# Layer 2: expert rows and router logits made group by group inside softmax attention, and row factors in place of two norms

## The chip, the cores and the metric

The kernel runs on one core of a Trainium2 chip. A core has a matrix engine (PE), a vector engine (DVE), an activation engine (ACT), a general engine (POOL) and a queueing engine (SP)[...]. They meet in on-chip memory (SBUF) and in the accumulator banks (PSUM) that PE writes. The metric is the device time of one execution in microseconds (us); the time before is the median of three runs.

## The reference, cut to what matters

The model has four layers over `x` of 2 sequences of 1024 rows with 128 features. Each layer computes `x = x + s * silu(f)` from the same `xn = layernorm(x)`, where `s` comes from a mixing branch and `f` from an expert branch. Layer 2, the only one that the change touches, is:

```python
# mixing branch: linear attention, 16 heads of 8
x_norm = (xn - mu) / sqrt(var + 1e-05) * ln_g + ln_b
q, k, v = split(x_norm @ w_qkv + b_qkv)
gate_sig = sigmoid(xn @ w_gate + b_gate)
gate_norm = gate_sig / (mean(gate_sig) + 1e-05)
q, k = elu(q * gate_norm) + 1, elu(k * gate_norm) + 1
out = (q . cumsum(k v)) / (q . cumsum(k) + 1e-05)
s = out @ w_proj + b_proj
# expert branch: softmax attention, then 2 of 8 experts
h = xn + attention(rms_norm(xn, norm1_w))      # rope, 16 query heads in 4 groups
logits = rms_norm(h, norm2_w) @ router_w + router_b
f = h + sum over the 2 chosen experts of weight * expert(rms_norm(h, norm2_w))
```

`rms_norm(x, w)` is `x / sqrt(mean(x * x) + 1e-06) * w`. The rope turns even features `xe` and odd features `xo`: `[xe*cos - xo*sin, xe*sin + xo*cos]`.

## The kernel before, in words

The 2048 rows lie as 16 tiles of 128 rows, `[128, 16, 128]` in SBUF; four tiles are a group (`G = 4`, groups 0 to 3), eight are a sequence. `layer2` works in three stages.

*Preparation.* `K.normalise` (L320) takes mean and variance of each group's rows on DVE (`moments`: L310, L311, then `rsqrt` L299 to L301, whose square root is on ACT), makes `xn`, and transposes it into `xT` on PE (L293). Then `Attention.prepare` runs for each sequence: the sum of squares of `xn` by ACT (`sumsq`, L333), its reciprocal root, `xw = xn * factor * norm1_w` on DVE (L1352), the rope as six POOL products and sums of 128x256 per group (L1360 to L1365), transposes of the turned rows `xr`, and the query, key and value products. PE starts on attention when the first sequence's two groups are there.

*Softmax attention* (`softmax_attention`). PE's order is written out by hand (`manual_schedule`): 72 steps, one for each block of 128 rows against 128 rows, 36 for each sequence. In a step PE makes score maxima's inputs in `pm` banks (pool `sm2`, three banks, all under the tag "pm"), DVE reduces each to `mx` (L1424), PE makes the scores `psc` (two buffers), ACT takes the exponential `pr` (L1468), and PE multiplies it by the values into `pat`. When a tile of rows is complete, `close` normalises it, projects it (`pho`) and adds it to `xn`: that is `h` (L1505), one tile after another; the last is tile 15. Parts that fall due in a later step are kept in the dictionary `later`. The other engines' orders come from a scheduler.

*Experts, with linear attention beside them.* After the last `h`, for each group: sum of squares of `h` on ACT (L333), its reciprocal root `rs`, `hn = h * rs * norm2_w` on DVE (L1031), a DMA of the four tiles of `hn` by SP into a table of rows in HBM (`keep_rows`, L1219), four transposes and a copy into `hnT` (L282 or L284, ACT and DVE in turn). The router's `logits` are 16 matmuls of 128x8 (`plg`) and one add into `lg` (L393). `top2` (its first maximum is `rm`, L364) and `Dispatch` make from them the places of each row (`dto`) and the rows of each place (`dfrom`, L1176). `d.n` = 23 blocks of experts follow (L1048 to L1078): two gathers of rows by POOL with `dfrom` (`xb`, L1188), their transpose, first products `p`, gate `sg` on ACT (L1069) and product `hh` on DVE (L1070), second product `po`, `yb` (L1076), and a scatter (L1198). `linear_attention` is a generator that the block loop advances at blocks 0, 0, 11 and 22. For each group it takes the second layer norm of `xn` again (`moments` with tag "la": L310, L311, `lars`; `xl`, L1242), transposes it (`pxl`, `xlT`), and makes `pqg` in two matmuls, 384 columns from `xlT` and 128 from `xT`; then `qg = pqg + bq` (L1255), the sigmoid `sig` with its sum (L1256), `qk` (L1263), the exponential (L1265), the products `kv` (L1280), their running sums `pcum` by matmul, `prod` (L1286) and the quotient.

Of the kernel before, what the change touches and what calls it, by code (L numbers as in the profile page):

```python
# [19 lines left out]
P = 128  # L20
# [252 lines left out]
class Kern:  # L273
# [46 lines left out]
    def normalise(self, pool, ps, x, xn, xT, xs=None):  # L320
        for g in range(NG):
            mv, rs = self.moments(pool, lambda j: x[:, g * G + j, :], G, 1e-5, "ln")
            for j in range(G):
                i = g * G + j
                self.nc.vector.tensor_scalar(xn[:, i, :], x[:, i, :], mv[:, j, 0:1], rs[:, j : j + 1], ALU.subtract, ALU.mult)  # L325
# [50 lines left out]
    def pair_softmax(self, pool, m1, m2):  # L376
# [9 lines left out]
        return w, d  # L386

# [606 lines left out]
def layer2(K, x, xn, xT, w, inp):  # L994
# [3 lines left out]
    with ExitStack() as es:  # L998
        keep = es.enter_context(tc.tile_pool(name="k2", bufs=1))
        s = keep.tile([P, NT, P], F32, name="s")  # L1000
        h = keep.tile([P, NT, P], F32, name="h")
        with ExitStack() as e1:
            pf = e1.enter_context(tc.tile_pool(name="f2", bufs=1))
            seqs = [Attention(K, pf, xn, w, h, b) for b in range(NB)]
            with tc.tile_pool(name="sn2", bufs=8, space=PSUM) as sn, tc.tile_pool(name="p2", bufs=1) as pp:
                K.normalise(pp, sn, x, xn, xT)
                for a in seqs:
                    a.prepare(pp, sn)
# [3 lines left out]
            with tc.manual_schedule(engines={mybir.EngineType.PE}):  # L1012
                with ExitStack() as e3:
# [3 lines left out]
                    softmax_attention(K, pf, sm, sc, so, seqs)  # L1017
        with ExitStack() as e2:
# [4 lines left out]
            hT = pf.tile([P, T], F32, name="hnT")  # L1023
            rs = pf.tile([P, NT], F32, name="rs")
            hn = pf.tile([P, NT, P], F32, name="hn")
            for g in range(NG):
                for i in range(g * G, g * G + G):
                    K.sumsq(pf, rs[:, i : i + 1], h[:, i, :])
                K.rsqrt(rs[:, g * G : (g + 1) * G], rs[:, g * G : (g + 1) * G], 1.0 / P, 1e-6)
                for i in range(g * G, g * G + G):  # L1030
                    nc.vector.scalar_tensor_tensor(hn[:, i, :], h[:, i, :], rs[:, i : i + 1], w["n2"], ALU.mult, ALU.mult)  # L1031
                keep_rows(K, inp["lists"][0], hn, g)
                K.to_feature_major(sf, lambda i: hn[:, i, :], hT, g)
            with tc.tile_pool(name="r2", bufs=1) as pr:
                (m1, h1), (m2, h2) = K.top2(pr, K.logits(pr, sf, hT, w["wr"], w["br"], 8), 8)
# [3 lines left out]
            linear = linear_attention(K, pa, sa, xn, xT, w, s)  # L1039
# [182 lines left out]
def linear_attention(K, pa, sa, xn, xT, w, s):  # L1222
# [7 lines left out]
    wq, bq = two("wq", [P, 384]), two("bq", [P, 512])  # L1230
# [4 lines left out]
    nc.vector.tensor_scalar_mul(wq, w["wqkv"], w["g"])  # L1235
# [595 lines left out]
```

## Time and profile before

| what | value |
|---|---|
| median of the runs | 1370.8 us (1363.27, 1370.8, 1372.84) |
| profiled execution: its own time, and its span | 1371.2 us, 1369.3 us |
| mean granted PE clock | 0.887 |
| busy share of the span: PE, DVE, ACT, POOL | 83%, 65%, 46%, 31% |
| layer 2: first rotation on POOL, first mask of attention, last `h` written | 490.99, 530.4, 843.84 us |
| layer 2: `lg` added, `dfrom` ready, first expert product `p` | 863.19, 911.34, 919.65 us |

All durations come from the profiled execution, whose span starts at 0; its own time is 1.9 us longer than its span. A line of the profile names the source line, the engine, the operation, then output and inputs by their names in the program with the shapes; "idle before" is how long the engine stood still in front of an instruction, and the arrow names what ended that. In a line in order of time the first number is the start, the second the duration; several instructions of one kind in a row are put together, with their count after "x". [...]

### The profile page before, as it was taken

How to read it: one execution, taken by the hardware profiler on the slowest of the kernel's cores; microseconds unless marked ns; L12 is line 12 of the kernel's file. 1: busy time of each engine (PE TensorE's matmuls, PEld its weight loads, DVE VectorE, ACT ScalarE, POOL GpSimd, SP SyncE). 2: the span in 40 equal slices, each digit the busy share in tenths (PEclk: the TensorE clock that was granted, in tenths of full speed). 3: DMA queues.
4: the chain of work that ended last, by engine and by line, in shares of the span. 5: the costliest groups of instructions: out<-in, count | busy, mean ns of one | idle time of the engine just before them, and what ended most of it. 6: DMA issues, size and time to landing. Idle time of an engine off the chain costs nothing. (4 is left out here: it accounts for less than half of the span.)

```text
span 1369.3 us, 19321 instructions
## 1 busy us (share of the span) xinstructions
PE 1134.2 (83%) x6861; PEld 793.5 (58%) x6861; DVE 885.1 (65%) x2216; ACT 634.7 (46%) x1072; POOL 425.2 (31%) x420
## 2 busy tenths in 40 slices
PE   5599866888898748999999998679989918799985
PEld 2277455787798425544444433458778815577664
DVE  6536445875665686577787753988657469566456
ACT  7665926215413232344455576233452316355761
POOL 0352160027455150000000000034766521467743
PEclk9899885899999757699999998769999967799997
DMA  2000003014344200000000000024344530233411
GB/s 89 0 1 1 0 15 122 1 59 157 105 136 134 62 0 1 1 1 1 1 1 1 1 1 24 8 89 117 111 131 126 155 104 24 70 85 96 78 54 47
DMA packets 49040, 75.72 MB, mean 55 GB/s; under 512 B 7335, under 2 KB 36402, under 8 KB 48688
## 3 DMA queue, kind: packets, MB, share of 16 engines
q1 hardware_dynamic: 39632, 54.30, 12.7%
q0 software_dynamic: 8448, 14.98, 5.0%
q10 hardware_dynamic: 864, 5.21, 1.1%
q8 instruction: 54, 0.88, 0.3%
q14 instruction: 42, 0.34, 0.1%
HBM read 63.95 MB, written 12.85 MB: 56 GB/s over the span
## 5 line engine op out<-in xcount | busy, mean ns | idle before, releaser
L1424 DVE TENSOR_REDUCE mx<-pm 128x1 f32<-128x512 f32 (+3 forms) x304 | 182.1, 656 | 65.6 <-PE pm L287 62.6
L1468 ACT ACTIVATE pr<-psc 128x1024 f32<-128x1024 f32 x144 | 139.6, 1021 | 103.9 <-PE psc L287 68.2
L1188 POOL DMA_INDIRECT xb<-xs,dfrom x132 | 131.7, 998 | 123.2 <-PE pxb L797 31.5
L1198 POOL DMA_INDIRECT ys<-yb,dto x132 | 137.0, 1038 | 95.3 <-DVE yb L1076 44.4
L1163 POOL TENSOR_TENSOR dhh<-dhh,w_c 128x1280 fp32r<-128x1280 f32 (+2 forms) x3 | 8.8, 2927 | 480.3 <-issue 385.6
L287 PE MATMUL pm<-kT,qT 32*128 32x128 f32 (+3 forms) x576 | 119.3, 364 | 15.5 <-DVE mx L1424 11.4
L287 PEld LDWEIGHTS pm<-kT,qT 32*128 32x128 f32 x576 | 68.8, 203 | 68.3 <-DVE mx L1424 48.2
L287 PE MATMUL p<-xbT,tw 128*128 128x256 f32 x368 | 100.6, 391 | 1.7 <-ACT sg L1069 1.4
L1069 ACT ACTIVATE sg<-p,tw 128x256 f32<-128x256 f32 x92 | 40.8, 472 | 94.9 <-PE p L287 87.2
L287 PE MATMUL pat<-pr,va 128*32 128x512 f32 x576 | 81.0, 630 | 0.2 <-ACT pr L1468 0.2
L293 PE MATMUL tp<-w_c,xn 128*128 128x128 f32 x64 | 19.5, 412 | 67.7 <-DVE xn L325 40.3
L287 PEld LDWEIGHTS p<-xbT,tw 128*128 128x128 f32 x368 | 63.4, 194 | 12.3 <-ACT sg L1069 3.5
L287 PE MATMUL psc<-qT,kT 32*128 32x512 f32 x288 | 64.8, 487 | 3.0 <-ACT pr L1468 3.0
L1070 DVE SCALAR_TENSOR_TENSOR hh<-p,tw,sg 128x256 f32<-128x256 f32 x92 | 42.6, 479 | 35.6 <-ACT sg L1069 24.0
L287 PEld LDWEIGHTS po<-tw,hh 128*128 128x128 f32 x368 | 54.6, 193 | 5.8 <-DVE hh L1070 1.1
L287 PE MATMUL po<-tw,hh 128*128 128x128 f32 x368 | 56.7, 277 | 0.4 <-DVE hh L1070 0.4
L293 PEld LDWEIGHTS tp<-w_c,xn 128*128 128x128 f32 x64 | 11.5, 187 | 75.8 <-issue 38.7
L287 PE MATMUL psc<-mT,onesR 32*128 32x512 f32 x288 | 54.5, 410 | 0.0
L282 ACT COPY xbT<-pxb 128x256 f32<-128x256 f32 (+3 forms) x38 | 15.2, 401 | 61.0 <-PE pxb L797 44.9
L287 PEld LDWEIGHTS psc<-qT,kT 32*128 32x128 f32 x288 | 31.4, 188 | 15.9 <-ACT pr L1468 13.6
L287 PE MATMUL pcum<-kv,w_c 128*128 128x512 f32 x64 | 35.3, 652 | 2.1 <-DVE prod L1286 1.6
L287 PE MATMUL pd<-uda,w_c 128*128 128x512 f32 x64 | 34.9, 647 | 0.9 <-ACT usz L517 0.9
(531 smaller groups left out, 2840.6 us busy)
## 6 DMA issues: line engine op xcount, KB each, us to landing
tw<-in_rows SPq DMA_DIRECT2D x23, 836.0 KB, 4.8
tw<-in_rows SPq DMA_DIRECT2D x39, 384.0 KB, 3.2
yt<-ys SPq DMA_DIRECT2D x24, 256.0 KB, 3.0
tw<-in_rows SPq DMA_DIRECT2D x47, 128.0 KB, 2.2
xb<-xs,dfrom POOLq DMA_INDIRECT x132, 3.3
ys<-yb,dto POOLq DMA_INDIRECT x132, 2.3
xs<-xn SPq DMA_DIRECT2D x8, 256.0 KB, 2.3
w_l<-in_l ACTq DMA_DIRECT2D x1, 1890.0 KB, 11.1
```

Of the source, the lines that this page charges most:

```text
L282: self.nc.scalar.copy(out, in_)
L287: self.nc.tensor.matmul(out, lhsT=lhsT, rhs=rhs, start=start, stop=stop)
L293: self.nc.tensor.transpose(pt[:, j, :], src(g * G + j), self.c["ident"])
L1069: nc.scalar.activation(sg, p1[:, k - k0, :], AF.Silu, bias=t[:, 1536 + k : 1537 + k])
L1070: nc.vector.scalar_tensor_tensor(hh[:, k, :], p2[:, k - k0, :], t[:, 1540 + k : 1541 + k], sg, ALU.add, ALU.mult)
L1163: nc.gpsimd.tensor_mul(h, h.bitcast(F32), c["slot"][:, at].unsqueeze(2).to_broadcast(shape))
L1188: self.K.nc.gpsimd.indirect_dma_start(dst, None, self.xs, bass.IndirectOffsetOnAxis(self.of_token[:, n : n + 1], 0))
L1198: d = self.K.nc.gpsimd.indirect_dma_start(self.ys, bass.IndirectOffsetOnAxis(self.to[:, n : n + 1], 0), src, None, bounds_check=2 * T - 1, ...
L1424: nc.vector.tensor_reduce(mx[:, starts.index(a), g, j : j + k], tile[0][:, : k * m].rearrange("p (j m) -> p j m", m=m), AX.X, ALU.max)
L1468: K.nc.scalar.activation(pr, ps, AF.Exp, scale=scale)
```

## The change

In preparation, `normalise` also keeps the mean square of each normalised row, `ms = variance * rs * rs`. `prepare` takes the root of that in place of the sums of squares; `norm1_w` is multiplied into four rope tables (cos and sin, for even and odd features) once on POOL, and `xw` becomes a scaled copy on ACT. The linear attention's own layer norm is left out: since `xn` has zero mean, its factor is `r2 = 1 / sqrt(ms + 1e-5)`, a number per row, applied after the product. So `pqg` is one matmul of 512 columns from `xT`, and `qg` is an add of 128 columns and a multiply-add of 384.

After attention's `h`, the rows `hn`, their DMA, their transposes and the router's logits are made group by group: groups 0 and 1 get their factors and rows at step 42, group 2 at step 52 (`norm`); transposes come at steps 45, 47 and 55 and logits at 48, 50 and 58, in `pm` banks, put into `later` through the new argument `fill`. Group 3 follows attention as before. The tiles `hT`, `rs`, `lg` and `hn` move to a pool that is open during attention, `hn` with two buffers of a group each.

```diff
@@ -317,9 +317,12 @@
         self.nc.vector.tensor_mul(out, mv[:, :, 1], rs)
         self.nc.vector.tensor_mul(out, out, rs)
 
-    def normalise(self, pool, ps, x, xn, xT, xs=None):
+    def normalise(self, pool, ps, x, xn, xT, xs=None, ms=None):
         for g in range(NG):
             mv, rs = self.moments(pool, lambda j: x[:, g * G + j, :], G, 1e-5, "ln")
+            if ms is not None:
+                self.mean_squares(ms[:, g * G : (g + 1) * G], mv, rs)
             for j in range(G):
                 i = g * G + j
                 self.nc.vector.tensor_scalar(xn[:, i, :], x[:, i, :], mv[:, j, 0:1], rs[:, j : j + 1], ALU.subtract, ALU.mult)
@@ -384,6 +387,14 @@
         nc.vector.reciprocal(w, w)
         nc.vector.tensor_mul(d, d, w)
         return w, d
+    def group_logits(self, ps, tag, lg, xT, g, w, bias, E):
+        pl = ps.tile([P, G, E], F32, name="plg", tag=tag)
+        for j in range(G):
+            i = g * G + j
+            self.mm(pl[:, j, :], xT[:, i * P : (i + 1) * P], w)
+        self.nc.vector.tensor_add(grp(lg, g), pl, bias.unsqueeze(1).to_broadcast([P, G, E]))
 
     def logits(self, pool, ps, xT, w, bias, E):
         pl = ps.tile([P, NT, E], F32, name="plg", tag="ps")
@@ -999,13 +1010,46 @@
         keep = es.enter_context(tc.tile_pool(name="k2", bufs=1))
         s = keep.tile([P, NT, P], F32, name="s")
         h = keep.tile([P, NT, P], F32, name="h")
+        hT = keep.tile([P, T], F32, name="hnT")
+        rs = keep.tile([P, NT], F32, name="rs")
+        lg = keep.tile([P, NT, 8], F32, name="lg")
+        r2 = keep.tile([P, NT], F32, name="r2")
+        normed = {}
+        def norm(gs):
+            for i in range(gs[0] * G, gs[-1] * G + G):
+                K.sumsq(keep, rs[:, i : i + 1], h[:, i, :])
+            at = slice(gs[0] * G, gs[-1] * G + G)
+            K.rsqrt(rs[:, at], rs[:, at], 1.0 / P, 1e-6)
+            for g in gs:
+                normed[g] = keep.tile(four, F32, name="hn", bufs=2)
+                for j in range(G):
+                    i = g * G + j
+                    nc.vector.scalar_tensor_tensor(normed[g][:, j, :], h[:, i, :], rs[:, i : i + 1], w["n2"], ALU.mult, ALU.mult)
+                nc.sync.dma_start(inp["lists"][0].rearrange("(i p) d -> p i d", p=P)[:, g * G : (g + 1) * G, :], normed[g])
+        def hidden_columns(g, ps, tag):
+            pt = ps.tile(four, F32, name="tp", tag=tag)
+            for j in range(G):
+                nc.tensor.transpose(pt[:, j, :], normed[g][:, j, :], c["ident"])
+            K.copy(hT[:, g * G * P : (g + 1) * G * P], flat(pt))
         with ExitStack() as e1:
             pf = e1.enter_context(tc.tile_pool(name="f2", bufs=1))
             seqs = [Attention(K, pf, xn, w, h, b) for b in range(NB)]
+            ms = keep.tile([P, NT], F32, name="ms")
             with tc.tile_pool(name="sn2", bufs=8, space=PSUM) as sn, tc.tile_pool(name="p2", bufs=1) as pp:
-                K.normalise(pp, sn, x, xn, xT)
+                n1 = w["n1"].rearrange("p (f two) -> p f two", two=2)
+                turn = {}
+                for n, a in (("cos", 0), ("sin", 0), ("cos", 1), ("sin", 1)):
+                    turn[n, a] = pp.tile([P, TPB, 64], F32, name=f"{n}{a}")
+                    nc.gpsimd.tensor_mul(turn[n, a], w[n], n1[:, :, a].unsqueeze(1).to_broadcast([P, TPB, 64]))
+                K.normalise(pp, sn, x, xn, xT, None, ms)
+                K.rsqrt(r2, ms, 1.0, 1e-5)
                 for a in seqs:
-                    a.prepare(pp, sn)
+                    a.prepare(pp, sn, ms, turn)
             pl = e1.enter_context(tc.tile_pool(name="l2", bufs=1))
             for a in seqs:
                 a.loop = pl
@@ -1014,29 +1058,28 @@
                     sm = e3.enter_context(tc.tile_pool(name="sm2", bufs=3, space=PSUM))
                     sc = e3.enter_context(tc.tile_pool(name="sc2", bufs=2, space=PSUM))
                     so = e3.enter_context(tc.tile_pool(name="so2", bufs=1, space=PSUM))
-                    softmax_attention(K, pf, sm, sc, so, seqs)
+                    half = TPB * (TPB + 1) // 2
+                    mid = half + G * (G + 1) // 2
+                    routed = [(half + 6, lambda: norm([0, 1])), (mid + 6, lambda: norm([2]))]
+                    for g, s0 in ((0, half + 9), (1, half + 11), (2, mid + 9)):
+                        routed.append((s0, lambda g=g: hidden_columns(g, sm, "pm")))
+                        routed.append((s0 + 3, lambda g=g: K.group_logits(sm, "pm", lg, hT, g, w["wr"], w["br"], 8)))
+                    softmax_attention(K, pf, sm, sc, so, seqs, routed)
         with ExitStack() as e2:
             pa = e2.enter_context(tc.tile_pool(name="a2", bufs=1))
             pf = e2.enter_context(tc.tile_pool(name="m2", bufs=1))
             sa = e2.enter_context(tc.tile_pool(name="sa2", bufs=3, space=PSUM))
             sf = e2.enter_context(tc.tile_pool(name="sf2", bufs=5, space=PSUM))
-            hT = pf.tile([P, T], F32, name="hnT")
-            rs = pf.tile([P, NT], F32, name="rs")
-            hn = pf.tile([P, NT, P], F32, name="hn")
-            for g in range(NG):
-                for i in range(g * G, g * G + G):
-                    K.sumsq(pf, rs[:, i : i + 1], h[:, i, :])
-                K.rsqrt(rs[:, g * G : (g + 1) * G], rs[:, g * G : (g + 1) * G], 1.0 / P, 1e-6)
-                for i in range(g * G, g * G + G):
-                    nc.vector.scalar_tensor_tensor(hn[:, i, :], h[:, i, :], rs[:, i : i + 1], w["n2"], ALU.mult, ALU.mult)
-                keep_rows(K, inp["lists"][0], hn, g)
-                K.to_feature_major(sf, lambda i: hn[:, i, :], hT, g)
+            norm([NG - 1])
+            hidden_columns(NG - 1, sf, "ps")
+            K.group_logits(sf, "ps", lg, hT, NG - 1, w["wr"], w["br"], 8)
             with tc.tile_pool(name="r2", bufs=1) as pr:
-                (m1, h1), (m2, h2) = K.top2(pr, K.logits(pr, sf, hT, w["wr"], w["br"], 8), 8)
+                (m1, h1), (m2, h2) = K.top2(pr, lg, 8)
                 d = Dispatch(K, pf, pr, sf, h1, h2, 8, 2 * P, inp["lists"])
                 w12 = K.pair_softmax(pf, m1, m2)
             pe = e2.enter_context(tc.tile_pool(name="e2", bufs=1))
-            linear = linear_attention(K, pa, sa, xn, xT, w, s)
+            linear = linear_attention(K, pa, sa, xT, r2, w, s)
             turns = [0, 0, d.n // 2, d.n - 1]
             loaded = {}
 
@@ -1219,7 +1262,7 @@
     K.nc.sync.dma_start(xs.rearrange("(i p) d -> p i d", p=P)[:, g * G : (g + 1) * G, :], grp(src, g))
 
 
-def linear_attention(K, pa, sa, xn, xT, w, s):
+def linear_attention(K, pa, sa, xT, r2, w, s):
 
 
 
@@ -1227,32 +1270,25 @@
     four = [P, G, P]
     two = lambda n, shape, bufs=1: pa.tile(shape, F32, name=n, tag=n, bufs=bufs)
 
-    wq, bq = two("wq", [P, 384]), two("bq", [P, 512])
+    wq, bq = two("wq", [P, 512]), two("bq", [P, 512])
     pb = sa.tile([P, 384], F32, name="pb", tag="ps")
     K.mm(pb, w["b"].to_broadcast([P, P]), w["wqkv"])
     nc.vector.tensor_add(bq[:, :384], pb, w["bqg"][:, :384])
     nc.scalar.copy(bq[:, 384:], w["bqg"][:, 384:])
-    nc.vector.tensor_scalar_mul(wq, w["wqkv"], w["g"])
+    nc.vector.tensor_scalar_mul(wq[:, :384], w["wqkv"], w["g"])
+    nc.scalar.copy(wq[:, 384:], w["wg"])
     for g in range(NG):
         first = g % (NG // NB) == 0
         kvs = nc.vector if g < NG // NB else nc.gpsimd
-        xl = two("xl", four)
-        mv, rs = K.moments(pa, lambda j: xn[:, g * G + j, :], G, 1e-5, "la")
-        for j in range(G):
-            nc.vector.tensor_scalar(xl[:, j, :], xn[:, g * G + j, :], mv[:, j, 0:1], rs[:, j : j + 1], ALU.subtract, ALU.mult)
-        pt = sa.tile(four, F32, name="pxl", tag="ps")
-        for j in range(G):
-            nc.tensor.transpose(pt[:, j, :], xl[:, j, :], c["ident"])
-        xlT = two("xlT", four)
-        K.copy(xlT, pt)
         qg = two("qg", [P, G, 512], 2)
         sig, gsum = two("sig", four), two("gsum", [P, G])
         for j in range(G):
             i = g * G + j
             pq = sa.tile([P, 512], F32, name="pqg", tag="ps")
-            K.mm(pq[:, :384], xlT[:, j, :], wq)
-            K.mm(pq[:, 384:], xT[:, i * P : (i + 1) * P], w["wg"])
-            nc.vector.tensor_add(qg[:, j, :], pq, bq)
+            K.mm(pq, xT[:, i * P : (i + 1) * P], wq)
+            nc.vector.tensor_add(qg[:, j, 384:], pq[:, 384:], bq[:, 384:])
+            nc.vector.scalar_tensor_tensor(qg[:, j, :384], pq[:, :384], r2[:, i : i + 1], bq[:, :384], ALU.mult, ALU.add)
             nc.scalar.activation(sig[:, j, :], qg[:, j, 384:], AF.Sigmoid, accum_out=gsum[:, j : j + 1])
 
         kvs.memset(qg[:, :, 384:400], 1.0)
@@ -1335,7 +1371,7 @@
         self.K.nc.scalar.copy(high, src)
         self.K.nc.vector.scalar_tensor_tensor(dst, high.bitcast(F32), low, src, ALU.mult, ALU.add)
 
-    def prepare(self, pp, sc):
+    def prepare(self, pp, sc, ms, turn):
         K, pf, xn, w, b = self.K, self.pf, self.xn, self.w, self.b
         nc, c = K.nc, K.c
         four = [P, G, P]
@@ -1344,24 +1380,22 @@
         for g in range(TPB // G):
             tiles = range(b * TPB + g * G, b * TPB + g * G + G)
             gr = rs[:, g * G : (g + 1) * G]
-            for j, i in enumerate(tiles):
-                K.sumsq(pp, gr[:, j : j + 1], xn[:, i, :])
-            K.rsqrt(gr, gr, 1.0 / P, 1e-6)
+            K.rsqrt(gr, ms[:, tiles.start : tiles.stop], 1.0, 1e-6)
             xw = pp.tile(four, F32, name="xw", bufs=2)
             for j, i in enumerate(tiles):
-                nc.vector.scalar_tensor_tensor(xw[:, j, :], xn[:, i, :], gr[:, j : j + 1], w["n1"], ALU.mult, ALU.mult)
+                nc.scalar.activation(xw[:, j, :], xn[:, i, :], AF.Copy, scale=gr[:, j : j + 1])
             pair = xw.rearrange("p t (f two) -> p t f two", two=2)
             xe, xo = pair[:, :, :, 0], pair[:, :, :, 1]
             at = slice(g * G, g * G + G)
-            cos, sin = w["cos"][:, at, :], w["sin"][:, at, :]
+            cose, sine, coso, sino = (turn[n, a][:, at, :] for a in range(2) for n in ("cos", "sin"))
             xr = pp.tile(four, F32, name="xr", bufs=2)
             t2 = pp.tile([P, G, 64], F32, name="t2", bufs=2)
             t3 = pp.tile([P, G, 64], F32, name="t3", bufs=2)
-            nc.gpsimd.tensor_mul(xr[:, :, :64], xe, cos)
-            nc.gpsimd.tensor_mul(t2, xo, sin)
+            nc.gpsimd.tensor_mul(xr[:, :, :64], xe, cose)
+            nc.gpsimd.tensor_mul(t2, xo, sino)
             nc.gpsimd.tensor_sub(xr[:, :, :64], xr[:, :, :64], t2)
-            nc.gpsimd.tensor_mul(xr[:, :, 64:], xe, sin)
-            nc.gpsimd.tensor_mul(t3, xo, cos)
+            nc.gpsimd.tensor_mul(xr[:, :, 64:], xe, sine)
+            nc.gpsimd.tensor_mul(t3, xo, coso)
             nc.gpsimd.tensor_add(xr[:, :, 64:], xr[:, :, 64:], t3)
             K.to_feature_major(sc, lambda i: xr[:, i % G, :], xrT, g)
         self.qT = qT = pf.tile([P, 4, SEQ], F32R, name="qT", bufs=2)
@@ -1507,7 +1541,7 @@
         return first, second, third
 
 
-def softmax_attention(K, pf, sm, sc, so, seqs):
+def softmax_attention(K, pf, sm, sc, so, seqs, fill):
 
 
 
@@ -1530,6 +1564,8 @@
         plan.append(dict(zip(("masked", "plain", "largest", "turn"), seqs[b].maxima(sb, shared, sm))))
         plan[-1]["due"] = first[n] - (2 if n < 3 else 3)
     later = {}
+    for s, part in fill:
+        later.setdefault(s, []).append(part)
 
     def take(kind, s, most):
 
```

## Prediction

> **What bounds the kernel now.** I read three views: the page for the whole, then busy time in chosen stretches of layer 2, then the order of time around the two places where the change cuts. From the page:
>
> ```profile
> PE 1134.2 (83%) x6861; PEld 793.5 (58%) x6861; DVE 885.1 (65%) x2216; ACT 634.7 (46%) x1072; POOL 425.2 (31%) x420
> L1424 DVE TENSOR_REDUCE mx<-pm 128x1 f32<-128x512 f32 (+3 forms) x304 | 182.1, 656 | 65.6 <-PE pm L287 62.6
> L287 PE MATMUL pm<-kT,qT 32*128 32x128 f32 (+3 forms) x576 | 119.3, 364 | 15.5 <-DVE mx L1424 11.4
> ```
>
> The matrix engine (PE) is the busiest, but the mean hides stages. Inside softmax attention PE and DVE feed each other through three `pm` banks: DVE takes a maximum out of a bank (656 ns), and most of PE's 15.5 us of idle time before `pm` ends on such a maximum. So what is queued in front of a maximum on DVE can stop PE. By stretches (the columns are length, then busy time and count of PE, PE's weight loads, DVE, ACT and POOL, then the granted PE clock):
>
> ```profile
> 484.00:500.00 16.00, 6.87 (x20) 3.66 (x20) 15.71 (x62) 8.13 (x41) 7.76 (x11) 0.50 0.00 0
> 531.00:650.00 119.00, 109.14 (x660) 58.43 (x660) 82.63 (x161) 44.73 (x53) 0.00 (x0) 0.80 0.00 1
> 650.00:760.00 110.00, 104.60 (x789) 53.15 (x789) 83.17 (x169) 57.93 (x69) 0.00 (x0) 1.00 0.00 1
> 760.00:844.00 84.00, 77.18 (x585) 32.12 (x585) 41.55 (x85) 56.45 (x67) 0.00 (x0) 1.00 0.01 1
> 864.00:912.00 48.00, 30.11 (x108) 19.32 (x108) 45.58 (x129) 12.53 (x22) 2.98 (x1) 0.72 0.14 54
> 912.00:1010.00 98.00, 92.06 (x499) 74.97 (x500) 71.95 (x155) 39.38 (x78) 58.34 (x56) 0.95 0.37 108
> ```
>
> Preparation (484 to 500) is DVE's, 98% busy. Attention (about 530 to 843.6) is PE's, 92 to 95%, at full clock from 650. From attention's end to 912 DVE is the bound again (95% from 864), while PE works 63% of the time at a clock of 0.72. The experts, from 912, are PE's. The change takes work out of the two DVE stretches and puts some into attention, where PE has nothing spare.
>
> **The stretch after attention: the gain.** Around its start and end, DVE and ACT in order of time (start, length):
>
> ```profile
> 843.55 0.29 DVE L1505 TENSOR_TENSOR h<-pho,xn 128x128 f32<-128x128 f32 x1 [1.27 <-PE pho L287]
> 845.92 1.28 ACT L300 ACT_TABLE_LOAD   x1
> 847.21 0.21 ACT L300 ACTIVATE rs<-rs 128x4 f32<-128x4 f32 x1
> 847.82 1.14 DVE L1031 SCALAR_TENSOR_TENSOR hn<-h,rs,w_l 128x128 f32<-128x128 f32 x4
> 863.19 0.26 DVE L393 TENSOR_TENSOR lg<-plg,w_l 128x128 f32<-128x128 f32 x1
> 864.95 0.28 DVE L364 TENSOR_REDUCE rm<-lg 128x16 f32<-128x128 f32 x1
> 911.15 0.19 DVE L1176 TENSOR_SCALAR dfrom<-dto 128x46 int32<-128x46 int32 x1
> ```
>
> The last `h` is done at 843.84, the router's logits `lg` are added at 863.19, its first maximum `rm` runs at 864.95, and the expert gather's indices `dfrom` are ready at 911.34; the gathers on POOL wait for those. So this is 67.5 us from `h` to `dfrom`, and every DVE instruction queued before `dfrom` counts. Going through both programs' DVE order between the last `h` and `dfrom`, the same dispatch and linear-attention work stands there, but these are gone: 16 `bn_stats` (3.75), 16 aggregates (1.6), the square root's small steps for four `lars` and three `rs` (2.3), 12 of 16 `hn` (3.4), 12 `xl` (3.4), one `hnT` copy and one `aT` copy that falls to ACT (1.4), 0.1 on `lg`: 16.0 us. Added: each `qg` add of 128x512 (0.68) becomes 128x128 (0.29) and 128x384 (the `bq` add of that size is 0.56), +0.17 x 8 = 1.4. Net 14.6 us of recorded durations; these overlap in the records (74.8 us of them fill some 62 us), so about **-12** if DVE alone sets the time.
>
> It doesn't at the start. By chain: the last tile's square ends at 844.3 (seven others no longer stand before it), table load 1.28, root 0.2, reciprocal and the `bq` add, `hn` x4 from 846.5 to 847.5. But PE's order now has `pb` and three 512-wide `pqg` before the four transposes, at half clock: 384+128 now start 1.8 us apart, so 845.4 + 3 x 1.8 = 850.8; transposes to 852.0, copy 852.7, the fourth `pqg` to 853.8, logits 854.8 (half of 1.9 at half clock). On DVE the sigmoid of the fourth tile, its sum and three `qk` stand before `rm`: about 856.1, 8.9 us earlier. From `rm` to `dfrom` 1.4 us of DVE is gone, so **-10.3**. I take -11.3, the middle, with ends -6 and -15. The DMA of `hn` to the table of rows for groups 0 to 2 moves into attention, where SP and DMA are idle (share 0.00); nothing waits for it until the gathers.
>
> **Attention: the price.** PE gets 12 transposes (four in 0.60 at full clock) and 12 logits matmuls (eight in 0.96): 1.8 + 1.4 = **+3.2 on the bound engine**. The rest is holes. `norm` is queued at step 42 behind tile 7's `h` (737.7 before) and at step 52 behind tile 11's. In DVE's queue: four maxima, the small scale of `rs`, its reciprocal (waiting for ACT's root), then eight `hn`, then again maxima. In ACT's queue: tile 7's square, a table load, the root (waiting for DVE's scale), a table load back, then two exponentials that before ran at 738.63. The scale can't run until the maxima end at 740.4, so root 740.6, Exp table 741.9, and those exponentials come 3.3 us late; DVE resumes maxima at 740.6 + 0.2 + 8 x 0.28 = 743.0. What stands behind: PE's next `psc` at 741.89 (waits for the exponentials) and its next `pm` banks (wait for the maxima). Between 736 and 748 DVE is idle for about 3 us in waits on PE, ACT for 6, so some is absorbed. I put PE's stall at 2.5 for the first and 1.0 for the second (half the `hn`), and 0.3 for the `pm` banks that transposes and logits hold: **+7.0** in all. Below: all holes covered, +3. Above: both holes in full (the late exponentials 3.3 and `hn` 2.3, then 3.3 and 1.1), 10.0, with the PE work, +13.2.
>
> [...] Here two roots are put between exponentials: four loads. [...]by the trace 4 x 1.28 = 5.1, since the root at 847.21 starts as the load at 845.92 ends, with nothing between. [...]
>
> **Preparation.** Sixteen squares leave ACT, sixteen `xw` leave DVE for it; four 128x512 products for the folded tables come onto POOL (1.1 to 1.3 us each by its other 128x512 products) before its first rotation.
>
> ```profile
> 489.64 1.12 DVE L1352 SCALAR_TENSOR_TENSOR xw<-xn,ars,w_l 128x128 f32<-128x128 f32 x4
> 490.99 0.74 POOL L1360 TENSOR_TENSOR xr<-xw,w_l 128x256 f32<-128x256 f32 x1 [9.96 <-DVE lnrs L301]
> 490.96 2.94 DVE L325 TENSOR_SCALAR xn<-x,lnmv,lnrs 128x128 f32<-128x128 f32 x4
> ```
>
> POOL idles 9.96 us before that rotation, so 4 x 1.2 = 4.8 us fit. But the tables now run beside DVE's casts and statistics, which moved behind the casts. [...]four `xn` take 2.94 beside rotations, 1.1 alone. If each of the four products held one DVE instruction up, preparation would be 4.8 late; by the rows, less DVE work (`xw`, 1.1 to 3.1 a group) returns as much. The first rotation comes at 491 to 494, the last of the second group at 503.8 to 505.4 against 504.3: **+0.3**, ends -4 and +5.
>
> **Experts.** Four transposes and copies of `xl` and four DVE `xl` fall after `dfrom`, about 0.6 us of PE, and some ACT work: **-1.5**, ends -3 and +1.5. Other layers are untouched.
>
> **Sum.** +0.3 + 7.0 - 11.3 - 1.5 = -5.5. The profiled execution took 1371.2 (span 1369.3), 0.4 above the median of 1370.8, so 1365.7 by either within half a microsecond. One per cent (13.7 us) is about what a measurement of this kernel can tell from no change; the three runs differ by 0.7%.
>
> **Rivals.**
> *The holes are covered and DVE's whole saving arrives.* Attention +3.5, the stretch after it -14.5, preparation -3 (ACT's squares, some 6 us, stood before the rotation), experts -3: -17, **1354**. For it: ACT idle 2.67 us and DVE 1.38 right after step 42. Against: PE's `pqg` order above.
> *The logits come earlier, `dfrom` does not.* If PE at its granted 0.72 paces the linear attention after `rm`, only -4 is left of -11.3: **1373**. For it: `pinv` is waited for 0.75 us just before `dfrom`. Against: DVE is 95% busy there, and it is PE that waits for DVE's `prod`, up to 2.2 us.
> *Slower: the clock.* PE idled 2.74 us before the transposes at 848.22, and the clock stood at half from 844 to 857.8. If each hole at the two roots costs such a stretch in attention, 14 us at half speed loses 7 us, twice: attention +21, total +8.5, **1379.7**. It decides from 11 us of lost full clock. Against: attention held full clock from 650 through PE waits of 0.3 us; holes of 2 us are near the 2.74.
> That the change doesn't move the work is excluded by the instruction order.
>
> **Numbers.** Forecast 0.45, first rival 0.28, second 0.17, clock 0.10. The sum's ends, combined, give 1357 to 1374; reaching into the rivals gives 1352 to 1377. Faster by over 1% (below 1357.1): most of the first rival and the forecast's edge, 0.29. Slower (above 1384.5): the clock's upper part, 0.07. Within: 0.64.
>
> **What would show it.** Right: `rm` some 9 us after the last `h` plus 3, near 12 us against 21; `h` to `dfrom` near 56 us against 67.5; attention 7 us longer, with DVE and ACT idle around two roots and a table load of 1.28 on each side. Wrong: attention longer by over 12 us or under 4; a clock below 1.00 between the roots; `dfrom` still 63 us after `h`; the second group's rotation off 504.3 by over 4 us.

## The result, and the profile after

The change made the kernel faster by half a per cent: median 1363.48 us (17 runs, 1357.54 to 1368.07) against 1371.55 us (17 runs of the kernel before beside them), ratio 0.9948, 95% interval 0.993 to 0.9966. That is 8.1 us less, where 5.5 were forecast. The profiled execution took 1359.4 us (span 1357.6), 11.8 less than that of before; some 4.7 us of it lie in front of layer 2 (layer 1's last add starts at 474.5 instead of 479.2), where nothing was changed, so I compare by stages of layer 2 and not by spans.

Page of the kernel after, the lines that answer to those of before:

```profile
PE 1127.9 (83%) x6813; PEld 785.5 (58%) x6813; DVE 878.1 (65%) x2169; ACT 633.0 (47%) x1051; POOL 428.9 (32%) x424
...
L1458 DVE TENSOR_REDUCE mx<-pm 128x1 f32<-128x512 f32 (+3 forms) x304 | 182.1, 656 | 65.2 <-PE pm L287 62.8
...
L287 PE MATMUL pm<-kT,qT 32*128 32x128 f32 (+3 forms) x576 | 118.9, 365 | 16.4 <-DVE mx L1458 12.5
```

Nothing on the page betrays what happened: the idle time before `pm` grew by 0.9 us. The stages tell more. Lengths in us, from the starts of these instructions: layer 1's last add to `x`; first mask of attention on PE; `h` of tile 7; `h` of tile 15; `dfrom`; layer 2's last add to `x`.

| profile | to the mask | to tile 7 | to tile 15 | to `dfrom` | to the last add | sum |
|---|---|---|---|---|---|---|
| before | 51.2 | 206.9 | 106.2 | 67.6 | 209.7 | 641.7 |
| after | 49.9 | 203.7 | 119.5 | 52.6 | 208.6 | 634.2 |
| difference | -1.4 | -3.2 | +13.3 | -15.0 | -1.2 | -7.5 |

So the stretch after attention gave 15 us, and attention took 13 of them back. A second profile of the change (e6_after below), taken from an execution of 1368.5 us, has 634.3 us for the same layer, so the two executions of the change differ outside it. The end of attention and the stretch behind it, in order of time (DVE and ACT of the kernel after; start, length):

```profile
847.57 0.29 DVE L1539 TENSOR_TENSOR h<-pho,xn 128x128 f32<-128x128 f32 x1 [1.26 <-PE pho L287]
848.39 1.28 ACT L300 ACT_TABLE_LOAD   x1
849.69 0.20 ACT L300 ACTIVATE rs<-rs 128x4 f32<-128x4 f32 x1
850.46 1.13 DVE L1029 SCALAR_TENSOR_TENSOR hn<-h,rs,w_l 128x128 f32<-128x128 f32 x4
855.51 0.19 DVE L397 TENSOR_TENSOR lg<-plg,w_l 128x32 f32<-128x32 f32 x1
856.80 0.28 DVE L367 TENSOR_REDUCE rm<-lg 128x16 f32<-128x128 f32 x1
900.16 0.19 DVE L1219 TENSOR_SCALAR dfrom<-dto 128x46 int32<-128x46 int32 x1
```

From the start of the last `h` to `rm` it is now 9.2 us (21.4 before), from `rm` to `dfrom` 43.4 (46.2 before).

What attention paid is seen around the first root, on ACT, DVE and PE:

```profile
728.10 0.28 DVE L1539 TENSOR_TENSOR h<-pho,xn 128x128 f32<-128x128 f32 x1
728.84 1.28 ACT L300 ACT_TABLE_LOAD   x1
729.38 0.16 DVE L299 TENSOR_SCALAR rs<-rs 128x8 f32<-128x8 f32 x1
730.36 1.28 ACT L1502 ACT_TABLE_LOAD   x1
730.38 0.20 DVE L301 RECIPROCAL rs<-rs 128x8 f32<-128x8 f32 x1 [0.83 <-ACT rs L300]
730.61 2.19 DVE L1029 SCALAR_TENSOR_TENSOR hn<-h,rs,w_l 128x128 f32<-128x128 f32 x8
732.72 1.88 DVE L1458 TENSOR_REDUCE mx<-pm 128x1 f32<-128x512 f32 x3
733.46 0.97 PE L287 MATMUL pmt<-identR,mp 128*128 128x128 f32 x4 [2.45 <-DVE mx L1458]
```

DVE is away from the maxima from 729.38 to 732.72, 3.3 us, and PE stands still for 2.45 us. At the second root PE stands still for 2.06 us, and then this is seen in its columns (kernel after, stretches of tiles 7 to 15; the number behind POOL's is the granted PE clock as a share of full speed, a mean of stretches at 0.50 and at 1.00, the only two values in these profiles):

```profile
728.10:735.00 6.90, 4.18 (x32) 2.60 (x32) 5.24 (x16) 5.65 (x8) 0.00 (x0) 0.90 0.26 76
735.00:745.00 10.00, 9.69 (x75) 5.59 (x76) 6.18 (x12) 5.18 (x9) 0.00 (x0) 0.90 0.01 2
745.00:774.00 29.00, 27.72 (x225) 15.64 (x221) 21.46 (x42) 16.21 (x23) 0.00 (x0) 1.00 0.00 1
774.00:795.90 21.90, 19.70 (x132) 8.93 (x132) 14.30 (x32) 13.96 (x18) 0.00 (x0) 0.77 0.04 13
795.90:847.90 52.00, 46.76 (x346) 17.83 (x341) 15.41 (x39) 36.94 (x49) 0.00 (x0) 1.00 0.00 1
```

Before, the clock was 1.00 through all of this. Lost full clock: 6.9 x 0.10 + 10 x 0.10 + 21.9 x 0.23 = 6.7 us. With 4.5 us of idle PE and some 3.5 us of added work (below) that makes 14.7; 13.3 were measured, so some of it overlaps. The same eight `pat` matmuls show the clock: the first line is behind the second root, the second is in the profile of before.

```profile
779.04 1.94 PE L287 MATMUL pat<-pr,va 128*32 128x512 f32 x8
```
```profile
779.40 1.06 PE L287 MATMUL pat<-pr,va 128*32 128x512 f32 x8
```

The DMA share of 0.26 beside the first root is the rows' DMA of groups 0 and 1; no wait in the trace ends on it.

### The profile page after: what moved, and what is told of

It is laid out like the page before. It is cut to its first block, busy times and chain, and to the rows that moved or that the text cites. A ratio compares the mean times of both kernels' runs of the same rounds, so it can differ in the third digit from the quotient of the medians.

```text
span 1357.6 us, 19123 instructions
## 1 busy us (share of the span) xinstructions
PE 1127.9 (83%) x6813; PEld 785.5 (58%) x6813; DVE 878.1 (65%) x2169; ACT 633.0 (47%) x1051; POOL 428.9 (32%) x424
## 3 DMA queue, kind: packets, MB, share of 16 engines
q1 hardware_dynamic: 39632, 54.30, 12.7%
```

## The experiments

My theory: the change gains in the DVE-bound stretch after attention and loses in attention, because DVE's and ACT's work for the two roots holds up the maxima and exponentials, PE runs dry, and its clock falls behind that. Rivals: PE's own added work and the shared `pm` banks are the price; ACT's table loads alone are; or one of the two parts of the change carries it and the other is idle. Runs e1 to e4 were on a chip on which the kernel before took some 4% longer (median 1422.6 us); each ratio is to runs of the kernel before on the same chip. Tiles 7 to 15 don't show that chip: e2 and e11, one kernel on two chips, both take 117.4 us there. The lengths of the stages inside layer 2, taken as above, in us:

| profile | ratio to before (interval) | to the mask | to tile 7 | to tile 15 | to `dfrom` | to the last add |
|---|---|---|---|---|---|---|
| e1_factors | 1.002 (0.9995 to 1.0046) | 50.3 | 216.8 | 111.0 | 54.8 | 215.0 |
| e2_routed | 1.0069 (1.0043 to 1.0095) | 51.4 | 208.0 | 117.4 | 55.3 | 220.8 |
| e3_poolrows | 0.9905 (0.9867 to 0.9942) | 50.5 | 204.3 | 112.5 | 52.6 | 215.1 |
| e4_newton | 0.9897 (0.9858 to 0.9935) | 50.2 | 204.3 | 109.6 | 52.9 | 213.1 |
| e5_factors_late | 0.9986 (0.997 to 1.0001) | 51.1 | 202.1 | 107.9 | 73.8 | 202.6 |
| e6_after | 0.9959 (0.994 to 0.9978) | 49.9 | 203.6 | 119.6 | 52.6 | 208.7 |
| e7_newton_casts | 0.9894 (0.9863 to 0.9926) | 49.5 | 204.5 | 109.6 | 52.9 | 208.1 |
| e8_newton_dead | 0.9903 (0.987 to 0.9936) | 49.7 | 203.8 | 110.4 | 53.0 | 206.7 |
| e9_tables_early | 0.9892 (0.9859 to 0.9924) | 46.9 | 209.5 | 110.9 | 53.0 | 207.5 |
| e10_before | one run | 51.2 | 211.1 | 106.3 | 67.1 | 208.9 |
| e11_routed_again | 1.0088 (1.0054 to 1.0123) | 51.2 | 208.0 | 117.4 | 54.6 | 219.0 |
| e12_one_hold | 0.9977 (0.996 to 0.9994) | 49.7 | 203.8 | 120.1 | 53.0 | 207.4 |

### The two parts by themselves

**e1_factors.** The routing is taken out of attention:

```diff
-                    softmax_attention(K, pf, sm, sc, so, seqs, routed)
+                    softmax_attention(K, pf, sm, sc, so, seqs, [])
...
-            norm([NG - 1])
-            hidden_columns(NG - 1, sf, "ps")
-            K.group_logits(sf, "ps", lg, hT, NG - 1, w["wr"], w["br"], 8)
+            for g in range(NG):
+                norm([g])
+                hidden_columns(g, sf, "ps")
+                K.group_logits(sf, "ps", lg, hT, g, w["wr"], w["br"], 8)
```

> Only the row factors (preparation and linear attention); rows, transposes and logits of all four groups come after attention again. Theory (the stretch after attention gains, attention pays 13 us for two holes of PE and the half clock behind them): attention as before, preparation -1, the stretch from the last h to dfrom shorter by about 7 us instead of 15 (9.4 us of DVE records gone, overlapping), so -8 us, ratio 0.994: as fast as the whole change. Rival (routing inside attention is what pays): stretch nearly as before, ratio 0.998.

Measured: no gain. The trace shows why it isn't the experiment that I meant: the rows' tiles lie in a pool that is open during attention, so the scheduler moved three roots with their table loads into attention by itself (rows at 639, 756 and 797 us). The stretch after attention is nearly as short as with the whole change (54.8), though two groups' transposes and three groups' logits are still in it; attention, from the mask to tile 15, is 14.7 us longer than before.

**e5_factors_late** repeats it with `hT`, `rs` and `hn` in the pool that opens after attention, as in the kernel before.

```diff
-        hT = keep.tile([P, T], F32, name="hnT")
-        rs = keep.tile([P, NT], F32, name="rs")
...
+            hT = pf.tile([P, T], F32, name="hnT")
+            rs = pf.tile([P, NT], F32, name="rs")
+            hn = pf.tile([P, NT, P], F32, name="hn")
```

> Only the row factors, and the rows' tiles lie in a pool that opens after attention, so that no root, square or row can be moved into attention (in the run e1_factors three norms with two table loads each had been moved there by the scheduler, at 639, 756 and 797 us). Theory (holes inside attention cost what the factors gain): no ACT_TABLE_LOAD between the first exponential and the last h; first maximum of the logits some 15 us after the last h (21 before, 9.8 in e1_factors), indices 45 us later; total -8 us, ratio 0.994. Rival (the factors gain nothing in themselves): ratio 1.00.

Measured: 0.9986, and the expectation of -8 us is wrong. Attention is free of roots (the 1.8 us that tiles 7 to 15 take more than before are one piece of 3.4 us at half clock, from 734.6), but the stretch grew to 73.8 us. ACT and PE of e5_factors_late in it:

```profile
849.08 1.28 ACT L300 ACT_TABLE_LOAD   x1
...
850.60 1.28 ACT L1272 ACT_TABLE_LOAD   x1
...
852.31 1.28 ACT L300 ACT_TABLE_LOAD   x1
...
854.30 1.28 ACT L1272 ACT_TABLE_LOAD   x1
```
```profile
854.34 1.88 PE L287 MATMUL plg<-w_l,hnT 128*128 128x8 f32 x8 [6.58 <-ACT hnT L282]
```

With the linear attention's norms gone, its sigmoids come so early that they alternate with the router's roots on ACT; each of the four changes of function shown comes with a table load of 1.28 us, PE waits 6.58 us for the copy that stands between them, and `rm` comes 29.7 us after the last `h` instead of 21.4. PE waits there because the logits come group by group, as in the change; the factors with all logits in one piece, as before, were not run, so what the factors are worth alone stays open. The later experts then are 7 us shorter; that more of the linear attention is already done fits this and was not tested.

**e2_routed** leaves preparation and linear attention as before and only routes inside attention (`normalise`, `prepare` and `linear_attention` are those of before).

```diff
-                K.normalise(pp, sn, x, xn, xT, None, ms)
-                K.rsqrt(r2, ms, 1.0, 1e-5)
+                K.normalise(pp, sn, x, xn, xT)
...
-            linear = linear_attention(K, pa, sa, xT, r2, w, s)
+            linear = linear_attention(K, pa, sa, xn, xT, w, s)
```

> Only the routing inside attention; preparation and linear attention as before the change. Theory: attention +13 us (PE idle 2.0 to 2.5 us at each of the two roots, clock below 1 behind each), stretch from the last h to dfrom -8 us (5.1 us of DVE records and the logits' chain), so about +5 us, ratio 1.004. Rival: the routing carries the gain: ratio 0.996.

Measured: 1.0069; on the other chip **e11_routed_again** gave 1.0088.

> e2_routed again, on this chip. If routing alone is a loss by itself: ratio 1.003 to 1.009, with two PE idles over 2 us at the roots. If the loss of e2_routed was that chip's: ratio 0.998 to 1.001.

The loss is not the chip's. Attention pays nearly as with the change (117.4; PE idle 2.46 and 2.07 us). The stretch gains 13 us, but the experts lose 9 of them again (219.0 against 209.7): the dispatch passed ahead of the linear attention, whose first group of `s` is written 3 us after `dfrom` (913.1) where it was 12 us before it (899.3). What was only pushed behind `dfrom` came back. With the change it stays in front (891.0 against 900.2): the linear attention's statistics and `xl`, 12 us of DVE durations between the last `h` and `dfrom` in the profile of before, are gone. So neither part gained much in these two forms: the factors without the routing gave some 2 us (e5, interval 0 to 4), the routing without the factors lost 10 to 12, and together they gain 6 to 8.

### The price inside attention

**e3_poolrows** makes the rows of groups 0 to 2 on POOL; roots and table loads stay on ACT.

```diff
-                    nc.vector.scalar_tensor_tensor(normed[g][:, j, :], h[:, i, :], rs[:, i : i + 1], w["n2"], ALU.mult, ALU.mult)
+                if g == NG - 1:
...
+                else:
+                    nc.gpsimd.tensor_mul(normed[g], grp(h, g), rs[:, g * G : (g + 1) * G].unsqueeze(2).to_broadcast(four))
+                    nc.gpsimd.tensor_mul(normed[g], normed[g], w["n2"].unsqueeze(1).to_broadcast(four))
```

> The whole change, but the rows hn of groups 0 to 2 are made on POOL (two products of 128x512 per group) and not on DVE; roots stay on ACT. Theory: the maxima no longer stand behind eight and four hn (2.2 and 1.1 us); the PE idle at the first root falls from 2.45 to under 1 us and at the second from 2.06 to about 1, the clock stays at 1.00 behind at least one of them; attention about 6 us shorter than with the change, ratio to before 0.990. Rival (ACT's table loads hold PE up, by the exponentials that come 3.3 us late): idle as with the change, ratio 0.995.

Measured: as the theory had it. PE idles 1.08 and 0.86 us, the clock stays at 1.00 from tile 7 to tile 15, which take 112.5 us instead of 119.5.

**e4_newton** also finds the roots on POOL, by nine Newton steps of four small POOL operations from a start of 0.05 (it suits the spread of this data), with transposes and logits three steps later.

```diff
-            K.rsqrt(rs[:, at], rs[:, at], 1.0 / P, 1e-6)
+            nc.gpsimd.tensor_mul(vh[:, at], rs[:, at], scale[:, at])
+            for n in range(9):
+                was = y if n else start
+                nc.gpsimd.tensor_mul(yy[:, at], was[:, at], was[:, at])
+                nc.gpsimd.tensor_mul(yy[:, at], yy[:, at], vh[:, at])
+                nc.gpsimd.tensor_sub(yy[:, at], three[:, at], yy[:, at])
+                nc.gpsimd.tensor_mul(y[:, at], was[:, at], yy[:, at])
```

> The whole change, but for groups 0 to 2 the reciprocal roots are found on POOL (nine Newton steps from a fixed start) and the rows hn made on POOL; no table load, no small DVE step and no hn inside attention; transposes and logits three steps later. Theory: no PE idle over 0.5 us at the roots' places, clock 1.00 from tile 6 to the last h; attention then only pays the 12 transposes and 12 logits matmuls and their copies, +4 us instead of +13; total about -17 us, ratio 0.988. Rival (pm banks held by transposes and logits, and PE's added work, are the price): attention still +11 or more, ratio 0.994.

Measured: 0.9897. Waits of PE from tile 7 to the end of attention in e4_newton (us in total, times, longest):

```profile
PE psc L287 <- ACT pr L1526: 3.1, 9, 0.4
PE pm L287 <- DVE mx L1482: 2.1, 9, 0.3
```

No wait on a maximum is longer than 0.3 us, and tiles 7 to 15 take 109.6 us. That is 3.4 more than before: 12 transposes, 12 logits matmuls and their banks are the whole price when nothing is held up (e7, with the same attention on another chip, has 109.6 too). The rival that they are the price is out.

**e8_newton_dead** adds to e4_newton eight dead DVE multiplications that read tile 7's `h` and four that read tile 11's, and **e12_one_hold** a single dead DVE product at each place instead. (Dead: nothing reads their results.)

```diff
# e8_newton_dead
+            for g in gs:
+                for j in range(G):
+                    nc.vector.tensor_scalar_mul(dead, h[:, at.stop - 1, :], 0.5)
# e12_one_hold
+            nc.vector.tensor_mul(dead, *[h[:, at.stop - 1, :].unsqueeze(1).to_broadcast([P, 24, P])] * 2)
```

> As e4_newton, with eight dead DVE multiplications of 128x128 that read tile 7's h, and four that read tile 11's, so that DVE alone is held up (2.2 and 1.1 us) and ACT loads no table. Theory (DVE's hold-up of the maxima is what stops PE): PE idle of 1 to 2 us behind tile 7's h and under 1 us behind tile 11's; no half clock where the idle is under 1.8 us; ratio 0.992. Rival (ACT's table loads are the cause): no idle over 0.6 us, ratio 0.990 as e4_newton.

> As e4_newton, with one dead DVE product of 128x3072 (about 3.3 us, as long as DVE was away from the maxima at the first root with the change) that reads tile 7's h, and one that reads tile 11's; ACT loads no table. Theory (an unbroken DVE hold-up of over 2 us stops PE, whatever its cause, and a PE idle of 2 us or more is followed by half clock): PE idle of 2 to 3 us behind both, the granted clock below 1.00 for 3 to 10 us behind each, tile 7 to tile 15 at 116 to 120 us instead of 109.6; ratio 0.995 to 0.997. Rival (it takes ACT's table loads too): idle under 1.8 us, clock 1.00, tile 7 to 15 at 111 to 114 us; ratio 0.991.

e8 missed the theory's expectation: no idle over 0.6 us at the roots' places, tiles 7 to 15 in 110.4. The scheduler had set maxima between the dead instructions; at most five of them stand in a row, 1.27 us. The single product of e12 is one instruction of 3.36 us (DVE, then PE behind it):

```profile
736.83 3.36 DVE L1031 TENSOR_TENSOR dead<-h 128x3072 f32<-128x3072 f32 x1
740.11 2.48 DVE L1485 TENSOR_REDUCE mx<-pm 128x4 f32<-128x512 f32 x4
```
```profile
740.84 0.79 PE L287 MATMUL pm<-kT,qT 32*128 32x512 f32 x1 [3.18 <-DVE mx L1485]
785.58 0.50 PE L287 MATMUL pm<-kT,qT 32*128 32x256 f32 x4 [1.74 <-DVE mx L1485]
```
```profile
740.80:745.10 4.30, 4.26 (x17) 2.15 (x18) 1.78 (x3) 0.52 (x1) 3.05 (x17) 0.50 0.00 0
785.50:794.00 8.50, 8.42 (x45) 4.63 (x45) 4.57 (x9) 2.11 (x3) 6.07 (x32) 0.56 0.01 2
```

PE idles 3.18 and 1.74 us, the clock stands at 0.50 and 0.56 behind it, and tiles 7 to 15 take 120.1 us: two unbroken hold-ups of DVE, with no table load at all, give back 10.5 us, as much as the change lost there. The twelve short ones of e8 cost 0.8. They are less work as well, 2.7 us of DVE against 6.7, so the two runs don't show what splitting alone is worth; but 10.5 us is more than the added work itself.

The runs put sizes on the loss of 9.9 us that the roots cost (119.5 less 109.6): table loads with rows on POOL 2.9 (e3 less e4; e3 also keeps two small DVE steps at each root, and its transposes come three steps earlier), DVE's rows in addition 7.0. On PE, the change idles 4.3 us longer than e4 in these tiles and runs 13.7 us of them at half clock, 6.8 us lost, where e4 runs none; the two make a little more than the 9.9.

The length of a stall alone doesn't tell whether the clock falls: stalls of 1.37 and 1.79 us in e1_factors, which ran before e8, left it at 1.00 (e8's expectation had put the limit at 1.8), one of 1.74 in e12 didn't. In all 14 profiles the clock changes only at times that lie whole multiples of 3.41 us apart. Two such slots of the change, around the second stall, and three of e1_factors, around its stall of 1.79 us (length, PE's work first, the clock behind POOL's numbers):

```profile
774.62:778.03 3.41, 1.64 (x17) 0.84 (x15) 1.85 (x7) 3.35 (x6) 0.00 (x0) 1.00 0.00 0
778.03:781.45 3.42, 3.13 (x13) 0.98 (x13) 2.13 (x4) 1.50 (x2) 0.00 (x0) 0.50 0.27 81
```
```profile
794.76:798.17 3.41, 2.47 (x19) 1.54 (x19) 1.56 (x7) 3.35 (x6) 0.00 (x0) 1.00 0.00 0
798.17:801.59 3.42, 2.58 (x25) 1.37 (x26) 2.71 (x6) 2.04 (x3) 0.00 (x0) 1.00 0.26 77
801.59:805.00 3.41, 3.27 (x32) 1.33 (x31) 3.27 (x9) 2.98 (x4) 0.00 (x0) 1.00 0.02 5
```

The longer idle time of the change lies within one slot, that of e1_factors is shared by two. From tile 7 to the last `h` the 14 profiles have 463 slots. In 13 of them PE worked for less than half of the slot (at most 1.67 us), and behind all 13 the clock was 0.50; behind the other 450 (2.05 us and more) it fell three times, once at the first stall of e12 and twice, for 3.4 us each, with no stall over 0.6 us near (e5 at 734.6, e9 at 784.0). So a stall explains the falls at the roots, but not every fall. How long the clock then stays down was not settled: the second stall of e2 and e11, 2.07 us, cost 3.4 us at half clock, that of the change, 2.06 us, cost 10.2.

### The preparation

**e7_newton_casts** moves the mask casts to ACT and the clearing of `mp` to POOL; **e9_tables_early** also makes the two cos tables before layer 1.

```diff
-        nc.vector.tensor_copy(shared[n], seqs[0].w[n].unsqueeze(1).to_broadcast(four))
+        nc.scalar.copy(shared[n], seqs[0].w[n].unsqueeze(1).to_broadcast(four))
...
-        nc.vector.memset(t.bitcast(F32), 0.0)
+        nc.gpsimd.memset(t.bitcast(F32), 0.0)
# e9_tables_early, ahead of layer1
+            for n, a in (("cos", 1), ("cos", 0)):
+                turn[n, a] = pool0.tile([P, TPB, 64], F32, name=f"{n}{a}") if a else w2[n]
+                nc.gpsimd.tensor_mul(turn[n, a], w2[n], n1[:, :, a].unsqueeze(1).to_broadcast([P, TPB, 64]))
```

> As e4_newton, and the casts of the masks go to ACT and the clearing of the mp tiles to POOL, so that the statistics of layer 2 don't stand behind them on DVE while POOL makes the rope tables (casts of 1.25 and 1.49 us with the change, 0.51 and 0.41 before). Theory: the first xn comes 5 us after the last add of layer 1 and not 9.5, the first mask of attention 3 us earlier, ratio 0.987. Rival (the rotations on POOL, not xn, set the start of attention): ratio as e4_newton, 0.990.

Measured: `xn` does come 4.6 us after the last add (9.5 with the change), but the first rotation only 0.7 us earlier (12.7 us after the last add, 13.5 with the change) and the mask 0.3: the rival was right. The tables now run beside `xn`. POOL and DVE of e7_newton_casts:

```profile
485.09 1.38 POOL L1072 TENSOR_TENSOR cos<-w_l 128x512 f32<-128x512 f32 x1
486.44 1.28 POOL L1072 TENSOR_TENSOR sin<-w_l 128x512 f32<-128x512 f32 x1
487.68 1.27 POOL L1072 TENSOR_TENSOR cos<-w_l 128x512 f32<-128x512 f32 x1
488.92 1.27 POOL L1072 TENSOR_TENSOR sin<-w_l 128x512 f32<-128x512 f32 x1
```
```profile
486.48 1.25 DVE L318 TENSOR_TENSOR ms<-ms,lnrs 128x4 f32<-128x4 f32 x1
487.65 1.38 DVE L328 TENSOR_SCALAR xn<-x,lnmv,lnrs 128x128 f32<-128x128 f32 x1
488.96 1.40 DVE L299 TENSOR_SCALAR ars<-ms 128x4 f32<-128x4 f32 x1
```

DVE's two steps on four columns took 1.25 and 1.40 us beside POOL products of 1.28 and 1.27 us (0.16 us without), and beside the last three of these products DVE's work went forward by one instruction for each, as the prediction had weighed it.

> As e7_newton_casts, but two of the four rope tables are made before layer 1 begins, so that only two POOL products of 1.3 us stand beside the first statistics and xn of layer 2. Theory (each POOL product of 128x512 holds one DVE instruction up: in e7_newton_casts a 128x4 step took 1.25 and 1.40 us beside the tables instead of 0.16): two such long steps instead of four or five, first rotation about 10 us after layer 1's last add instead of 12.7, first mask of attention some 2.5 us earlier; ratio 0.988. Rival (POOL's own clearing of va and mp, 3.8 us, sets the first rotation): ratio 0.989 as e7_newton_casts.

Measured: the mask is 2.7 us earlier than in e7_newton_casts, as expected, but the ratio is the same, 0.9892: the way from mask to tile 7 took 209.5 us instead of 204.5. The 5 us are lost clock: 54.6 us at half there, against 44.4. What set them is open. **e10_before** is a second profile of the kernel before.

> The kernel before, for a second profile of it. If half clock at attention's start is the chip's and not the kernel's, it shows half clock for some 40 to 50 us behind the first mask again, none from tile 6 on, and the stretch from the last h to the indices again near 67.5 us.

The half clock behind the mask and the stretch after attention (67.1) are there again. But there is more half clock on the way to tile 7 (58.0 us against 47.8, with a last piece at 657 to 667 us), and that way is 211.1 us, 4.2 more than in the first profile. This one execution took 1382.1 us, more than all 12 others of its kernel on that chip (1364.1 to 1374.9), so it bounds little.

The versions with the roots and rows on POOL (e4, e7, e9) are the fastest, some 1% faster than before and, timed on one chip, 0.65% faster than the change (e7 0.9894 against e6 0.9959). They don't differ among each other by more than their intervals.

## Why the prediction was right, and where its terms were not

Forecast were 1365.7 us and a change within 1%; measured were 1363.5 us and -0.5%. Direction and case were right, but terms of the sum were off and partly cancelled, so the closeness is in part luck: from tile 7 on attention cost 6.3 us more than was put for it, while the stretch after it (-3.7), the way to tile 7 (-3.2) and preparation (-1.7) came out better. Two things that the prediction had named as signs of being wrong did come: attention over 12 us longer (13.3 from tile 7 on; 10.1 from the mask on) and a clock below 1.00 between the roots.

- *The stretch after attention* was the gain and has the mechanism described, but -15.0 us instead of -11.3, as much as the first rival had (-14.5). The term "three 512-wide `pqg` at half clock, 1.8 us apart" failed: they ran at full clock, three in 3.06 us, so `rm` came 9.2 us after the last `h` and not 12.3. From `rm` to `dfrom` 2.8 us went, and not 1.4; no run took that apart. The rival "logits earlier, `dfrom` not" didn't occur; e2 and e11 show another loss where the linear attention keeps its norms: `dfrom` comes early, and the experts pay.
- *PE's added work*, +3.2: 3.4 in e4_newton.
- *The holes* were put at 3.8 us; they cost 9.9. The first stall was right (2.5, measured 2.45). The second was put at 1.0 by "half the `hn`", and was 2.06: the maxima wait for the root at least as long as at the first (DVE stands 1.35 us in front of the reciprocal, 0.83 at the first), whatever the number of rows. And the clock behind the holes was put at nothing; it lost 6.7 us. It stood in the prediction as the slower rival, with a chance of 0.10; what came is a fair half of it (6.7 of 14 us), at the place and for the cause named there. Here 0.50 followed stalls of 2.06 and 2.45 us, and one of 1.74 in e12; in the two slots of 3.41 us in front of the change's falls PE worked 1.64 and 0.96 us. The prediction's own evidence for this rival was misread: in the profile of before the clock falls at 844.0, and PE's 2.74 us begin only at 845.5.
- *The table loads* took 1.28 us each at the roots shown, as the trace of before had it, and the root starts as the load ends (848.39 + 1.28 = 849.67, root at 849.69).
- *Preparation*, -1.4 for +0.3, in two large parts: `xn` came 4.6 us later behind the last add (9.5 against 4.9), and `xn` to the mask went from 46.3 to 40.3 us, more than the sum had given the squares and `xw` for. The 4.6 is close to the 4.8 that was weighed for four held-up instructions, but is made otherwise: beside the tables the two mask casts took 1.25 and 1.49 us (0.51 and 0.41 before), which is 1.8, and the first statistics now stand behind the casts and the clearing of `mp` on DVE. In e7, where both are off DVE, `xn` is back at 4.6 us with the tables still beside it.
- *Experts*, -1.2 for -1.5.
- *Not forecast:* -3.2 us between the mask and tile 7. The 1273 matmuls there are the same; the granted clock was 0.90 instead of 0.88 (41.0 us at half instead of 47.8, 3.4 us of lost clock). Both profiles of the change have 203.6 to 203.7 us, those of before 206.9 and 211.1. What sets the clock there was not settled, and no run took it apart; so these 3.2 of the 7.5 us can't be put down to the change with certainty.

## What to carry to other kernels

For work that is moved beside a bound engine, look at the longest unbroken time for which it keeps a feeder away, and not at its sum alone: twelve small DVE instructions, 2.7 us in all and at most 1.3 in a row, cost 0.8 us; two of 3.4 us at the same places cost 10.5, since PE ran dry for 3.2 and 1.7 us and then went on at a clock of 0.50 and 0.56. Giving work to POOL, idle in this stretch with the change (0.00 us busy), took 7.0 (e3) and 9.9 us (e4) of the loss away here; keeping its pieces short is the other thing to try. Look at the granted clock behind every stall of the matrix engine. And test the parts of a change together as well as alone: here one part by itself lost 10 to 12 us, the other gained some 2, and both gained 6 to 8.

## What the runs showed of the hardware that I had not expected

- In these 14 profiles the clock is 0.50 or 1.00 and changes only on a grid of 3.41 us; PE stalls of 2.45 and 2.06 us with the change were followed by 3.4 and 10.2 us at 0.50, and half clock came with stalls of 3.18 and 1.74 us in e12 too.
- In e7, DVE instructions on 128x4 elements took 1.25 and 1.40 us beside POOL products of 128x512, for 0.16 alone.
- Between the mask and tile 7, where 41.0 us are at half clock with the change, one kernel took nearly the same time in both of its profiles (208.0 us twice for the routed one, on two chips; 203.6 and 203.7 for the change), while e7 and e9, whose instructions in that stretch are the same, differ by 5 us (44.4 us at half against 54.6); only the kernel before differed between its two profiles (206.9 and 211.1).
